# Perceiver layer on one core: x's keys as one product, softmax sums through DRAM, gating and late scan placed anew

## The chip, the cores and the metric

The kernel runs on one core of one Trainium2 chip. A core has TensorE (PE in the profile, with its weight loads as PEld), VectorE (DVE), ScalarE (ACT), GpSimd (POOL) and SyncE (SP), each with its own instruction stream that runs in order. The metric is the time of one execution on the device in microseconds; less is better.

## The reference, cut to what matters

One layer: cross-attention of 256 tokens of each of four batches to 4096 context tokens and to themselves, then a router that sends a quarter of the tokens of each batch to a small self-attention and the rest through a state-space model (SSM), then a mixture of experts. All in fp32.

```python
# x (4,256,256), ctx (4,4096,256); layernorm before each part, residual after it
q = split_heads(x1 @ Wq1)                        # 8 heads of 64
k = concat([x1 @ Wk1, ctx @ Wk2])                # 256 keys of x, 4096 of ctx
v = concat([x1 @ Wv1, ctx @ Wv2])
x = x + softmax(q @ k.T * 64**-0.5) @ v @ Wo + bo

score = gelu(xn @ r_w1 + r_b1) @ r_w2 + r_b2      # router
top 64 tokens of a batch: attention of 16 heads; the 192 others: SSM
    xc = silu(conv(xi)); h = exp(delta*A) * h + delta*xc*B; y = sum_s C*h   # 16 states

g, u = x @ w_gate[e].T, x @ w_up[e].T             # 8 experts, the best 2 per token
x = x + sum_e weight[e] * (silu(g) * u) @ w_down[e].T
```

## The kernel before, in words

**Attention.** The 4 batches times 4 head pairs make 16 groups G. A group has 8 steps s of 32 query rows, so 128 steps n in all; the loop from L1509 on writes out the order of every engine by hand, and each engine runs its instructions in that order. In a step, the products of `scores` fill the PSUM tile `su` with the scores of both heads j, each against the four quarters q of the keys: 1024 keys of ctx per quarter from `kt[r, q, lo : lo + 512]` (L1383, contraction over the 64 rows of one head) and 64 keys of x per quarter (L1391). For the latter, `qz` holds q with the other head's rows zero (`[P, 2, T]`, filled at L1351 by `k_self`), so that the contraction runs over all 128 rows. `copy_max` (L1403, DVE) copies the scores to SBUF and takes the maximum, `stat` (L1410, L1415, L1420) joins the maxima of the four quarters through a product, `exps` (L1431, ACT) takes the exponentials with their sums, `turn` (L1440, DVE) transposes them, and `values` (L1449, PE) multiplies by v four steps at a time. Between these lie pieces of the next group's work: `k_chunk` (keys, L1330), `v_chunk` (values, L1367), `k_self` (keys and queries of x).

At the end of a group, `sums` (in step s=0 of the next group) adds the parts of the softmax sums with a small product (L1463), takes the reciprocal `rl` (64 rows, 8 steps; L1468) and spreads it along a diagonal, `dg` (L1470). `spread` (at s=1) multiplies `dg` by the constant `pair`, which gives the reciprocals in PSUM as `psr`, one row per output channel and one column per query (L1477). `normalize` (L1492, DVE) multiplies the two halves of the attention output `ao` by it; `project` (L1496) follows.

**Work in the background.** Routers, small attentions and SSMs of finished batches are generators. They yield a delay and a budget in the time of a planner, `now`, which the loop moves on by a fixed cost for each piece that it places; `slot(budget)` places as many due items as the budget allows. So the planner's numbers set the order in the instruction streams, not the time on the chip. Batches 0 to 2 run beside the attention; batch 3 runs "late", beside the experts.

**Experts.** `ordered()` takes six of the eight token tiles, sorted by expert, in NB=19 blocks of 128: per block a gather of the tokens (`gather`, POOL), a turn (`turn_block`, PE L1723, ACT L1726), the gate products p0b and the up products p1b (both L1732, `half`, each 8 products), the gating `gated` (tanh on ACT L1678, then DVE `sg` L1679 and `hb` L1683), and the down products pdb of the block before (L1746, `down`) with their store `ysd` on ACT's queue (L1754). The PSUM tiles of the products come from a pool of three (`ps_g`). The last two tiles, those of batch 3, go through all experts densely (`experts()`, pg and pu L1868, pde L1881), once batch 3's router, attention and SSM are done. After each product half the loop adds its cost to `now` and calls `slot(5.0)`, which places the late work of batch 3: layernorm and router (psxn L250, psh L270, pssc L277), the ranks (two comparisons, one per half of the tokens; DVE), psn (L306 to L308), the gathering products psg (L331), psin (L626), then 16 pieces of the scan: `decay` on ACT (L805), and on DVE a product L838, the scan L839, a product L845 and a sum L846; `sums` adds a piece into the PSUM tile `yps` (L813). Then follow the SSM's output (pssd L871, psback L881) and the dense tiles' layernorm and transpose (`prepare`: x4l, psx L1824).

Of the kernel before, what the change touches and what calls it, by code (L numbers as in the profile page):

```python
# [8 lines left out]
F32 = mybir.dt.float32  # L9
# [5 lines left out]
P = 128  # L15
# [31 lines left out]
def perceiver_layer(ctx: ExitStack, tc: tile.TileContext, a: dict, out: bass.AP):  # L47
# [184 lines left out]
    def router(b, st):  # L232
# [55 lines left out]
        for h in range(2):  # L288
# [8 lines left out]
            if h == 0 and not late:  # L297
                yield 0.5, 1.6
# [4 lines left out]
        yield (4.5 if late else 1.0), 1.4  # L303
# [299 lines left out]
    def front_late(b, st, ws, conv):  # L603
# [73 lines left out]
        yield 5.4, 0  # L677
# [99 lines left out]
    def ssm_scan_late(b, st):  # L777
# [45 lines left out]
        zero = pool.tile([P, SG, NBOT], F32, tag="dbl", name="zero", bufs=4)[:, :2]  # L823
# [10 lines left out]
        for i in range(K * NDT):  # L834
            k, m = divmod(i, NDT)
            decay(i + 1)
            db = dbl[i] = pool.tile([P, SG, NBOT], F32, tag="dbl", name="db", bufs=4)
# [9 lines left out]
            if i:  # L847
                sums(i - 1)
# [4 lines left out]
            yield 3.9, 3.8  # L853
# [351 lines left out]
    with ExitStack() as s1:  # L1205
# [85 lines left out]
        def turn_x(b):  # L1291
# [11 lines left out]


        pair = fin.tile([2 * 32, P], F32, name="pair")
        nc.vector.tensor_copy(
            pair.rearrange("p (j d) -> p j d", j=2), bc(quarter[: 2 * 32, 0:2, 0], 2, HD)
        )
        qzs = [fin.tile([P, 2, T], F32, name=f"qz{i}") for i in range(2)]
        for t in qzs:  # L1310
            nc.gpsimd.memset(t, 0.0)
# [11 lines left out]
        def k_chunk(G, g):  # L1323
            b = G // NHP
            if G not in kts:
                kts[G] = wke.tile([P, 4, QK], F32, tag="kt", name="kt")
# [9 lines left out]
        def k_self(G):  # L1336
            x1T = x1Ts[G // NHP]
            if G not in kts:
                kts[G] = wke.tile([P, 4, QK], F32, tag="kt", name="kt")
# [7 lines left out]
            keys_out(G, SQ, ps[:, :T])  # L1347
            qTs[G] = qzs[G % 2]
            for j in range(2):
                r = slice(j * HD, (j + 1) * HD)  # L1350
                nc.scalar.activation(qTs[G][r, j, :], ps[r, T:], AF.Copy, scale=HD ** -0.5)  # L1351
# [24 lines left out]
        def scores(n):  # L1376
            G, s = divmod(n, 8)
            qT, kt = qTs[G], kts[G]
            for lo in range(0, SQ, 512):
                for q in range(4):  # L1380
                    for j in range(2):
# [3 lines left out]
                            qT[r, j, s * 32 : (s + 1) * 32], kt[r, q, lo : lo + 512],  # L1385
# [3 lines left out]
            for j in range(2):  # L1389
                for q in range(4):  # L1390
                    nc.tensor.matmul(  # L1391
                        su[q * 32 : (q + 1) * 32, SX[j] : SX[j] + QK - SQ],
                        qT[:, j, s * 32 : (s + 1) * 32], kt[:, q, SQ:],
                        start=True, stop=True,
                    )
# [60 lines left out]
        dgs, rss = {}, {}  # L1456

        def sums(G):
# [8 lines left out]
            rl = fin.tile([2 * 32, 8], F32, tag="rl", name="rl")  # L1467
            nc.vector.reciprocal(rl, ps[: 2 * 32, :8])  # L1468
            dgs[G] = fin.tile([2 * 32, 8, 32], F32, tag="dg", name="dg")
# [483 lines left out]
```

## Time and profile before

| | before |
|---|---|
| time, median of 3 runs (lowest to highest) | 1538.34 us (1537.46 to 1538.44) |
| profiled execution: its time, its span | 1534.16 us, 1532.4 us |
| mean granted TensorE clock in it | 0.984 |
| busy, PE / DVE / ACT / POOL | 1452.4 / 1062.5 / 758.1 / 411.9 us |
| PE instructions | 15686 |
| moved by DMA | 223.41 MB, mean 146 GB/s |

The span is the time from the first to the last instruction of the profiled execution. Attention takes it up to some 1245 us, its end and the last projection to 1273 us, and experts with batch 3's background work take the rest. Busy time is the sum of an engine's instructions; the slices cut the span in 40 equal parts of 38.3 us and give busy time in tenths. In a row of groups, "idle before" is time in which the engine stood still just before such an instruction, with the one that released it.

### The profile page before, as it was taken

Reading aid. Unit: us, or ns where it says so; the run is one execution under the profiler, and the core shown is the slowest. Engines: PE = TensorE matmul, PEld = TensorE weight load, DVE = VectorE, ACT = ScalarE, POOL = GpSimd, SP = SyncE. Lnnn points to the kernel's source line nnn. Section 1 sums busy time; section 2 is a strip of 40 time slices with the busy share of each in tenths; the row PEclk is TensorE's granted clock in tenths of the full one; section 3 lists DMA queues with packets and bytes.
Section 4 is the critical chain, followed back from the end, with each engine's and each line's share of the span. In section 5 each row is a group of like instructions: output and inputs, shape, how many; then the busy total and the mean of one; then the engine's idle time right before and its main releaser. Section 6 shows DMA issues by size and latency. Waiting matters only on the chain.

```text
span 1532.4 us, 37303 instructions
## 1 busy us (share of the span) xinstructions
PE 1452.4 (95%) x15686; PEld 1034.5 (68%) x15686; DVE 1062.5 (69%) x1825; ACT 758.1 (49%) x1484; POOL 411.9 (27%) x465
## 2 busy tenths in 40 slices
PE   7999999999999999999999999999998968899899
PEld 3657676677666566675756665757574757888687
DVE  1666665656589986565899956666999663689453
ACT  3444454455566645454766544656655523544211
POOL 1000000000069960000499800001999101210110
PEclk9999999999999999999999999999999979999999
DMA  6455434424345443424445444352643333788461
GB/s 229 142 158 152 157 116 150 154 85 131 109 145 179 138 131 121 148 82 144 144 135 174 135 134 130 103 163 73 182 157 99 105 131 109 244 272 283 136 203 49
DMA packets 157767, 223.41 MB, mean 146 GB/s; under 512 B 14976, under 2 KB 76160, under 8 KB 157600
## 3 DMA queue, kind: packets, MB, share of 16 engines
q1 hardware_dynamic: 149632, 208.96, 43.3%
q10 hardware_dynamic: 6480, 8.00, 1.6%
q0 software_dynamic: 1488, 4.07, 1.0%
q8 instruction: 124, 2.03, 0.5%
q14 instruction: 43, 0.35, 0.1%
HBM read 216.56 MB, written 4.42 MB: 144 GB/s over the span
## 4 chain that ended last, share of the span: by engine, by line
PE 65%; POOL 15%; DVE 11%; issue 4%; ACT 2%; DMA 1%; SPq 0%; ACTq 0%; DVEq 0%; POOLq 0%
PE po L1449 12%; PE su L1383 11%; PE psv L1367 11%; PE psk L1330 9%; POOL y L751 6%; POOL db L736 5%; POOL db L749 5%; DVE sp L1403 3%; PE su L1391 2%; PE pg L1868 2%; PE pu L1868 2%; PE pde L1881 2%; PE p1b L1732 2%; DVE db L743 1%; DVE pt L1440 1%
## 5 line engine op out<-in xcount | busy, mean ns | idle before, releaser
L1403 DVE TENSOR_SCALAR_CACHE_REDUCE sp<-su 128x1088 f32<-128x1088 f32 x256 | 318.8, 1282 | 181.9 <-PE su L1391 181.9
L1440 DVE STREAM_TRANSPOSE pt<-sp 128x1088 f32<-128x1088 f32 x256 | 328.0, 1295 | 57.4 <-PE po L1449 57.4
L1431 ACT ACTIVATE sp<-sp,nb 128x1088 f32<-128x1088 f32 x256 | 305.1, 1195 | 13.4 <-DVE nb L1420 13.2
L1449 PE MATMUL po<-pt,v 128*64 128x128 f32 x4352 | 261.9, 277 | 2.3 <-DVE pt L1440 1.3
L1383 PE MATMUL su<-kt,qz 64*32 64x512 f32 x4096 | 255.5, 607 | 4.4 <-DVE nb L1420 3.7
L1330 PE MATMUL psk<-ctx,wk 128*128 128x512 f32 x512 | 245.5, 612 | 10.5 <-DMA ctx<-in_ctxT 7.8
L1367 PE MATMUL psv<-wv,ctx 128*128 128x128 f32 x2048 | 250.3, 279 | 0.5 <-DMA ctx<-in_ctxT 0.3
L1449 PEld LDWEIGHTS po<-pt,v 128*64 128x64 f32 x4352 | 240.0, 138 | 13.9 <-issue 7.5
L1367 PEld LDWEIGHTS psv<-wv,ctx 128*128 128x128 f32 x2048 | 236.1, 192 | 6.6 <-issue 1.3
L1330 PEld LDWEIGHTS psk<-ctx,wk 128*128 128x128 f32 x512 | 91.4, 192 | 95.6 <-issue 86.0
L1318 ACT COPY kt<-psk 128x512 f32<-128x512 f32 x128 | 74.9, 585 | 157.7 <-PE psk L1330 157.5
L1383 PEld LDWEIGHTS su<-kt,qz 64*32 64x32 f32 x4096 | 63.3, 107 | 123.6 <-issue 94.3
L751 POOL TENSOR_TENSOR y<-y,db 128x192 f32<-128x192 f32 x192 | 135.5, 706 | 15.1
L1371 ACT COPY v<-psv 128x512 f32<-128x512 f32 x144 | 79.3, 558 | 119.4 <-PE psv L1367 118.0
L743 DVE TENSOR_TENSOR_SCAN db<-da,db 128x384 f32<-128x384 f32 x96 | 122.7, 1279 | 13.2 <-POOL db L736 2.5
L749 POOL TENSOR_TENSOR db<-db,cb 128x384 f32<-128x384 f32 x96 | 111.3, 1159 | 24.3 <-DVE da L741 24.3
L395 POOL TENSOR_TENSOR kbd<-qk,hmask 128x512 f32<-128x512 f32 x8 | 9.1, 1156 | 402.6 <-ACT qk L385 402.6
L736 POOL TENSOR_TENSOR db<-bb,xc 128x384 f32<-128x384 f32 x96 | 111.2, 1180 | 0.2
L1391 PEld LDWEIGHTS su<-kt,qz 128*32 128x32 f32 x2048 | 34.5, 109 | 108.9 <-issue 108.9
L731 ACT ACTIVATE da<-delta,A_log_sb 128x192 f32<-128x192 f32 x192 | 75.6, 447 | 52.7 <-DVE da L741 39.7
L1486 ACT COPY ao<-po 128x128 f32<-128x128 f32 x32 | 8.5, 264 | 149.8 <-PE po L1449 149.8
L1415 PEld LDWEIGHTS su<-mq,same 128*128 128x128 f32 x256 | 41.1, 192 | 54.8 <-DVE mq L1410 37.0
(298 smaller groups left out, 1582.1 us busy)
## 6 DMA issues: line engine op xcount, KB each, us to landing
ctx<-in_ctxT SPq DMA_DIRECT2D x256, 512.0 KB, 5.0
gateT<-in_gateT SPq DMA_DIRECT2D x27, 512.0 KB, 4.6
upT<-in_upT SPq DMA_DIRECT2D x27, 512.0 KB, 4.7
downT<-in_downT SPq DMA_DIRECT2D x27, 512.0 KB, 5.7
bb<-bcd SPq DMA_DIRECT2D x24, 192.0 KB, 3.8
cb<-bcd SPq DMA_DIRECT2D x24, 192.0 KB, 3.9
wv<-in_wv SPq DMA_DIRECT2D x32, 128.0 KB, 2.5
in_w<-in_in_w SPq DMA_DIRECT2D x32, 128.0 KB, 2.4
```

The costliest lines, as they stand in the source:

```text
L736: nc.gpsimd.tensor_tensor(db, bbs[k], bc(xc[:, m, :], 1, SG), ALU.mult)
L743: nc.vector.tensor_tensor_scan(out=db, data0=da, data1=db, initial=0.0, op0=ALU.mult, op1=ALU.add,)
L749: nc.gpsimd.tensor_tensor(db, db, cbs[k], ALU.mult)
L751: nc.gpsimd.tensor_tensor(y[:, m, :], y[:, m, :], db[:, s, :], ALU.add)
L1330: nc.tensor.matmul(ps, wqk[G][:, 0, c, :], ct[:, c, :], start=(c == 0), stop=(c == KD - 1),)
L1367: nc.tensor.matmul(ps[:, i * P : (i + 1) * P], lhsT, wv[G][:, w, c, :], start=(c == 0), stop=(c == KD - 1),)
L1371: nc.scalar.copy(v.rearrange("p k d -> p (k d)"), ps[:, : n * P])
L1383: nc.tensor.matmul(su[q * 32 : (q + 1) * 32, SC[j] + lo : SC[j] + lo + 512], qT[r, j, s * 32 : (s + 1) * 32], kt[r, q, lo : lo + 512], sta ...
L1403: nc.vector.tensor_scalar(out=sps[n][j], in0=su[:, SU[j] : SU[j] + QK], scalar1=1.0, scalar2=None, op0=ALU.mult, op1=ALU.max, accum_out=nm ...
L1431: nc.scalar.activation(sps[n][j], sps[n][j], AF.Exp, bias=nbs[n][:, j : j + 1], accum_out=lss[b][:, hp, s, j : j + 1],)
L1440: nc.vector.transpose(pts[m, j][:, i, :], sps[n][j])
L1449: nc.tensor.matmul(pos[m][j * HD : (j + 1) * HD, :], vts[m // 2, k // 4][:, k % 4, j * HD : (j + 1) * HD], pts[m, j][:, :, kk * 32 : (kk + ...
```

## The change

It has six parts.

1. q is kept unpadded (`qh`), and the keys of x go to zero-padded tiles `kxs`, one block of columns per head. One product per quarter then gives the scores of both heads, 128 columns wide, written with a stride through `middle` to the places in `su` where they lay before. `kt` holds the keys of ctx alone.
2. The reciprocals of the sums no longer go through `dg`, `pair` and a product. `sums` transposes `rl` in blocks of 32x32 on DVE, `spread` (now at s=0) writes it to a DRAM tile `rd` with two DMAs on ACT's queue, and the new `fetch` (at s=1) reads it back, each head's row repeated over its 64 partitions, into the SBUF tile `rs` which `normalize` reads.
3. In `ordered()`, the tanh and `sg` are placed after the first half of the up products instead of after all of them and the start of `down`; only the product `hb` stays there.
4. `ordered()` is started, up to its first turn, before the slot that precedes the blocks.
5. The late ranks are placed in two parts, with delays of 0.9 and 2.7 in place of one of 4.5.
6. The late scan starts after 3.6 instead of 5.4, its pieces are 3.5 apart instead of 3.9, each piece's `sums` come two pieces later instead of one, and the buffers `dbl` are five instead of four.

```diff
@@ -294,13 +294,13 @@
             nc.vector.tensor_reduce(out=rank[:, h : h + 1], in_=eq, axis=AX.X, op=ALU.add)
-            if h == 0 and not late:
-                yield 0.5, 1.6
+            if h == 0:
+                yield (0.9 if late else 0.5), 1.6
         top = small.tile([P, 2], F32, name="top")
...
         )
-        yield (4.5 if late else 1.0), 1.4
+        yield (2.7 if late else 1.0), 1.4
@@ -674,7 +674,7 @@
         next(st["late"])
-        yield 5.4, 0
+        yield 3.6, 0
         u = st["u"] = pool.tile([P, NDT, NBOT], F32, tag="ul", name="ul")
@@ -820,7 +820,7 @@
         yps = st["yps"] = late["psum"].tile([P, 2, 512], F32, name="yps")
-        zero = pool.tile([P, SG, NBOT], F32, tag="dbl", name="zero", bufs=4)[:, :2]
+        zero = pool.tile([P, SG, NBOT], F32, tag="dbl", name="zero", bufs=5)[:, :2]
         nc.gpsimd.memset(zero, 0.0)
@@ -834,7 +834,7 @@
             decay(i + 1)
-            db = dbl[i] = pool.tile([P, SG, NBOT], F32, tag="dbl", name="db", bufs=4)
+            db = dbl[i] = pool.tile([P, SG, NBOT], F32, tag="dbl", name="db", bufs=5)
             nc.vector.tensor_tensor(db, spread[k, 0], bc(u[:, m, :], 1, SG), ALU.mult)
@@ -844,13 +844,14 @@
             nc.vector.tensor_tensor(db[:, : SG // 2], db[:, : SG // 2], db[:, SG // 2 :], ALU.add)
-            if i:
-                sums(i - 1)
+            if i > 1:
+                sums(i - 2)
             if m == NDT - 1:
...
                 start(gate_late(b, st))
-            yield 3.9, 3.8
+            yield 3.5, 3.8
+        sums(K * NDT - 2)
         sums(K * NDT - 1)
@@ -1301,13 +1302,12 @@
-        pair = fin.tile([2 * 32, P], F32, name="pair")
-        nc.vector.tensor_copy(
-            pair.rearrange("p (j d) -> p j d", j=2), bc(quarter[: 2 * 32, 0:2, 0], 2, HD)
-        )
-        qzs = [fin.tile([P, 2, T], F32, name=f"qz{i}") for i in range(2)]
-        for t in qzs:
+        middle = su[:, SX[0] : SX[0] + 2 * (SX[1] - SX[0])].rearrange("p (j k) -> p j k", j=2)
+        qhs = [fin.tile([P, T], F32, name=f"qh{i}") for i in range(2)]
+        kxs = [fin.tile([P, 4, 2, QK - SQ], F32, name=f"kx{i}") for i in range(2)]
+        for t in kxs:
             nc.gpsimd.memset(t, 0.0)
@@ -1323,7 +1323,7 @@
             if G not in kts:
-                kts[G] = wke.tile([P, 4, QK], F32, tag="kt", name="kt")
+                kts[G] = wke.tile([P, 4, SQ], F32, tag="kt", name="kt")
             ct = load_ctx(b, g)
@@ -1335,8 +1335,6 @@
             x1T = x1Ts[G // NHP]
-            if G not in kts:
-                kts[G] = wke.tile([P, 4, QK], F32, tag="kt", name="kt")
             ps = ps_m.tile([P, 512], F32, tag="m", name="psks")
@@ -1344,11 +1342,14 @@
                     )
-            keys_out(G, SQ, ps[:, :T])
-            qTs[G] = qzs[G % 2]
+            qTs[G] = qhs[G % 2]
+            nc.scalar.activation(qTs[G], ps[:, T:], AF.Copy, scale=HD ** -0.5)
             for j in range(2):
                 r = slice(j * HD, (j + 1) * HD)
-                nc.scalar.activation(qTs[G][r, j, :], ps[r, T:], AF.Copy, scale=HD ** -0.5)
+                nc.scalar.copy(
+                    kxs[G % 2][r, :, j, :].rearrange("p q (k i) -> p q k i", i=32),
+                    ps[r, :T].rearrange("p (k q i) -> p q k i", q=4, i=32),
+                )
@@ -1382,17 +1383,16 @@
                             su[q * 32 : (q + 1) * 32, SC[j] + lo : SC[j] + lo + 512],
-                            qT[r, j, s * 32 : (s + 1) * 32], kt[r, q, lo : lo + 512],
+                            qT[r, s * 32 : (s + 1) * 32], kt[r, q, lo : lo + 512],
                             start=True, stop=True,
...
-            for j in range(2):
-                for q in range(4):
-                    nc.tensor.matmul(
-                        su[q * 32 : (q + 1) * 32, SX[j] : SX[j] + QK - SQ],
-                        qT[:, j, s * 32 : (s + 1) * 32], kt[:, q, SQ:],
-                        start=True, stop=True,
-                    )
+            for q in range(4):
+                nc.tensor.matmul(
+                    middle[q * 32 : (q + 1) * 32, :, : QK - SQ],
+                    qT[:, s * 32 : (s + 1) * 32], kxs[G % 2][:, q],
+                    start=True, stop=True,
+                )
@@ -1453,7 +1453,10 @@
-        dgs, rss = {}, {}
+        rts, rds, rss = {}, {}, {}
+        rls = [fin.tile([2 * 32, 32], F32, name=f"rl{i}") for i in range(2)]
+        for t in rls:
+            nc.gpsimd.memset(t, 0.0)
@@ -1464,18 +1467,25 @@
                 )
-            rl = fin.tile([2 * 32, 8], F32, tag="rl", name="rl")
-            nc.vector.reciprocal(rl, ps[: 2 * 32, :8])
-            dgs[G] = fin.tile([2 * 32, 8, 32], F32, tag="dg", name="dg")
-            nc.vector.tensor_tensor(
-                dgs[G], bc(rl, 2, 32), bc(dm[: 2 * 32, :], 1, 8), ALU.mult
-            )
+            rl = rls[G % 2]
+            nc.vector.reciprocal(rl[:, :8], ps[: 2 * 32, :8])
+            rts[G] = fin.tile([2 * 32, 32], F32, tag="rt", name="rt")
+            nc.vector.transpose(rts[G], rl)
...
-            rss[G] = bank("psr")[:, :T]
-            nc.tensor.matmul(
-                rss[G], pair, dgs[G].rearrange("p s i -> p (s i)"), start=True, stop=True
+            rd = dram.tile([2, 8, 32], F32, tag="rd", name="rd")
+            for j in range(2):
+                nc.scalar.dma_start(out=rd[j], in_=rts[G][j * 32 : j * 32 + 8, :])
+            rds[G] = rd
+        def fetch(G):
+            rss[G] = fin.tile([P, T], F32, tag="rs", name="rs")
+            nc.scalar.dma_start(
+                out=rss[G],
+                in_=rds[G].rearrange("j s i -> j (s i)").unsqueeze(1).to_broadcast([2, HD, T]),
             )
@@ -1594,13 +1604,14 @@
                     piece(2)
+                    if s == 0 and n:
+                        spread(G - 1)
                     slot(2.9)
...
                     last = s == 1 and G
+                    slot(1.5)
                     if last:
-                        spread(G - 1)
-                        now[0] += 0.6
-                    slot(1.5)
+                        fetch(G - 1)
                     piece(1)
@@ -1672,7 +1683,7 @@
-        def gated(pg, pu, out, n):
+        def silu(pg, n):
@@ -1680,7 +1691,10 @@
             )
-            nc.vector.tensor_tensor(out, sg[:, :n], pu[:, :n], ALU.mult)
+            return sg
+        def gated(pg, pu, out, n):
+            nc.vector.tensor_tensor(out, silu(pg, n)[:, :n], pu[:, :n], ALU.mult)
@@ -1760,10 +1774,19 @@
             turn_block(0)
+            yield 0.0
             for j in range(NB):
...
                 load(j + 3, 0)
-                pu = yield from half(j, 1)
+                up = half(j, 1)
+                yield next(up)
+                sg = silu(pg, 512)
+                try:
+                    while True:
+                        yield next(up)
+                except StopIteration as end:
+                    pu = end.value
                 load(j + 3, 1)
@@ -1771,7 +1794,9 @@
                 hs[j] = fk.tile([P, NHC, P], F32, name="hb")
-                gated(pg, pu, hs[j].rearrange("p m i -> p (m i)"), 512)
+                nc.vector.tensor_tensor(
+                    hs[j].rearrange("p m i -> p (m i)"), sg, pu, ALU.mult
+                )
                 yield from rest
@@ -1894,9 +1919,11 @@
         late["prepare"] = prepare
+        blocks = ordered()
+        next(blocks)
         now[0] += 1.0
         slot(5.0)
-        for took in ordered():
+        for took in blocks:
             now[0] += took
```

## The prediction

> **What bounds the kernel now.** I read the engine totals and the slices first, then the chain, then the groups by form, then the timeline of one attention step and of the tail.
>
> ```profile
> PE 1452.4 (95%) x15686; PEld 1034.5 (68%) x15686; DVE 1062.5 (69%) x1825; ACT 758.1 (49%) x1484; POOL 411.9 (27%) x465
> PE   7999999999999999999999999999998968899899
> POOL 1000000000069960000499800001999101210110
> PE 65%; POOL 15%; DVE 11%; issue 4%; ACT 2%; DMA 1%; SPq 0%; ACTq 0%; DVEq 0%; POOLq 0%
> ```
>
> TensorE is at work in 95% of the span. So there are two ways to gain: give PE less to do, or fill its idle time (80 us). POOL's 15% of the chain lies in the three stretches where its slices read 9: the scans of batches 0 to 2 beside the attention. There a wait can end on VectorE or POOL, and a shorter PE may gain nothing. Listing the gaps between PE records after 1273 us gives 20.2 us of idle in the tail (experts, with batch 3's scan beside them). The waits name most of it:
>
> ```profile
> PE p1b L1732 <- DVE sg L1679: 7.2, 5, 3.5
> PE psx L1824 <- ACT x4l L211: 3.6, 2, 3.4
> PE yps L813 <- DVE db L846: 3.4, 1, 3.4
> ```
>
> An attention step, at the turn of a group (s=0 to s=1, timeline at 300 us):
>
> ```profile
> 309.39 0.43 PE L1391 MATMUL su<-kt,qz 128*32 128x64 f32 x16
> 309.75 2.19 PE L1449 MATMUL po<-pt,v 128*64 128x128 f32 x36
> 311.87 0.70 PE L1477 MATMUL psr<-dg,pair 64*128 64x256 f32 x2
> 312.50 2.19 PE L1449 MATMUL po<-pt,v 128*64 128x128 f32 x36
> 315.12 0.28 DVE L1492 TENSOR_TENSOR ao<-ao,psr 128x128 f32<-128x128 f32 x1
> 318.57 1.95 PE L1383 MATMUL su<-kt,qz 64*32 64x512 f32 x32
> 318.75 2.50 DVE L1440 STREAM_TRANSPOSE pt<-sp 128x1088 f32<-128x1088 f32 x2 [3.35 <-PE po L1449]
> ```
>
> PE goes from product to product without a pause. `normalize` runs at 315.12, and VectorE's next work, the turns, can't begin before PE has ended `po` at 318.6.
>
> **The change part by part.** Durations are from the profiled execution: 1534.16 us, span 1532.4, 1.8 us around it. It lies 4.2 us below the median of the runs, 1538.34; I sum against 1534.16 and carry the difference to the median.
>
> *1. x's keys in one product.* The rows are
>
> ```profile
> L1391 PE MATMUL su<-kt,qz 128*32 128x64 f32 x2048 | 55.1, 225 | 0.0
> L1383 PE MATMUL su<-kt,qz 64*32 64x512 f32 x4096 | 255.5, 607 | 4.4 <-DVE nb L1420 3.7 <-ACT qz L1351 0.7
> L1351 ACT ACTIVATE qz<-psks 64x256 f32<-64x256 f32 x32 | 12.1, 378 | 0.3
> ```
>
> fp32 products are two records each. Per step 16 records of 64 columns take 309.39 to 309.75 = 0.36 us, in four waves of four column tiles; the change makes 8 records of 128 columns, two waves. Columns streamed: 4x64 before, 2x128 after, the same. L1383 gives the price of a column: 32 records in 1.87 us (307.52 to 309.39), eight at a time, so 4 x 512 columns, 0.91 ns each, 0.12 us per 128. By columns the old step is 0.23 us and 0.13 of start and drain, and the new step is again 0.36: gain 0. By count of waves (0.09 each) it would be 0.18: gain 0.18 x 128 steps = 23 us. The Trainium skill has a rule here, "TensorEngine Tiling (Array Packing)", section "Instruction Overhead": each product has about 60 cycles of overhead, so that one of 1 column lasts as long as one of 60. At 64 columns the old products are just above that floor, so by the rule too streaming sets the time, gain 0, if the overheads of the four column tiles overlap; if they add, most of the 23 us. The two ends are far apart; the nearest row is L1383, which goes by columns. I take 2 us (0.015 a step, one wave start less), keep 0 to 23. A loss is excluded on PE: no column or record more. ACT per group: one `kt` copy (364 ns) and two `qz` (378) become one `qh` of the first form and two `kx` of the second, 1.12 us before and after. Clearing kxs for qz is on POOL once, at the start.
>
> *2. Sums through memory.* Off PE: psr, 311.87 to 312.50 = 0.63 us a group, x16 = 10.1 us, all of it in PE's line of work. Off DVE: dg (507 ns), on DVE a 64x32 transpose; its own row doesn't exist, but the 128x1088 one is 1295 ns for 17 times the elements and twice the partitions, so 0.1 to 0.2 us; 0.3 us saved, worth nothing by itself. `normalize` reads SBUF instead of PSUM, 261 ns kept. On ACT's queue come three DMA issues, two writes (8 rows of 128 bytes) at s=0 and the fetch at s=1; ACT's issues in this trace are 0.34 us (`ysd`, `bcd`), so 1.0 us a group. Behind the writes on ACT stand the exponentials of n-1 (308.1 to 311.6): 0.7 us later, they end at 312.3, and the turns that read them don't start before 318.75. Hidden. If rt were late they would wait for it, but the reciprocal is done at 305.9 and ACT comes to the writes after 307.6. The fetch waits for the writes' landing in ACT's in-order queue; nothing due stands behind it until the copy of `ao` at 318.72. The planner's shift of 0.6 us for psr goes with it; in the attention it moves no other instruction.
>
> Then the landing. The new wait is `normalize` for rs, and behind it on DVE stand both turns, the next copy_max and mq, for which PE's L1415 waits (already its largest wait, 18.9 us in 14 times). The fetch is issued at about 312.4 and must have landed by 318.4: 6 us. How long does it take? Rows:
>
> ```profile
> wv<-in_wv SPq DMA_DIRECT2D x32, 128.0 KB, 2.5
> bb<-bcd SPq DMA_DIRECT2D x24, 192.0 KB, 3.8
> ctx<-in_ctxT SPq DMA_DIRECT2D x256, 512.0 KB, 5.0
> ```
>
> The same 128 KB as wv: 2.5 us. But a rule of the Trainium skill speaks against it: "DMA: Bandwidth & Descriptors", section "Why a DMA increments its semaphore by 16 and not by 1", says that the number of engines is the largest, up to 16, that divides the slowest dimension of both access patterns. The fetch's source has 2 (head), then 64 (repeat), then 256: two engines with 64 packets of 1 KB each. Packets of 1 KB take 46 to 49 ns in this trace, so 3 us in a row instead of 0.4: landing 2.5 + 2.6 = about 5 us by the rule, 2.5 by the row; no run here shows which. With ctx traffic on the same two engines it is up to 8. At 5 us it lands at 317.4, and `normalize` ends 1 us before the turns can start: nothing is lost in a quiet group. In the six groups whose psr lies in POOL's stretches (475.6, 548.8, 792.3, 865.6, 1110.7, 1182.0) DVE has no pause there, so half of their 0.63 is taken to be lost: 1.9. At the attention's end psr ran at 1261.9 and `normalize` right behind it, with `project` waiting (psx at 1264.6); writes and fetch in a row end between 1262 and 1266: 1 us lost (0 to 3). Sum: -10.1 + 1.9 + 1 = -7.2; bounds -10 to +14 (1.3 us a group lost, were landing 8 us).
>
> *3. Gating in two steps.* p1b waits for DVE's sg because p0b's bank comes free late (three banks). The tanh and the first product now come after a quarter of `up` instead of after all of it, some 1.3 us earlier in PE's order, and DVE reads p0b before the scan pieces that stood ahead of it. DVE's work is the same two products (682 and 688 ns). Of the five waits (3.53, 1.53, 1.30, 0.46, 0.38) all may go: -7.2.
>
> *4. Start of the blocks, ranks, scan pieces.* `next(blocks)` ahead of a slot puts the first turn's copy before a table load: 1.96 us idle at 1273 gone, but psxn then waits for xn: -0.6. Ranks in two: psn, which needs `top` from DVE, goes ahead of psxb and pdb on PE and waits for it: +2.5 (0 to 3.5), and the branch's front is 3 us earlier. Sums two pieces behind instead of one: the 3.37 us wait for db goes (there POOL's kbd stretched two DVE operations from 0.96 and 0.56 to 1.61 and 1.28 us; with another piece between that is covered). About three expert blocks now lie behind the last piece, 5.5 us of PE each, and cover the chain pssd, psback, x4l: 0.87 + 0.46 + 3.40 + 0.17 + 0.68 = -5.6. In return the scan is denser: a piece comes every 4 planner steps rather than 5. A piece is 0.95 + 1.76 + 0.97 + 0.56 = 4.3 us of DVE, and two thirds of a block beside it 0.9: 5.2 us of DVE against about 4.3 of PE. DVE, 88 of 97 us busy there before, becomes the bound:
>
> ```profile
> 1330.00:1427.00 97.00, 89.29 (x643) 82.64 (x643) 88.06 (x99) 40.91 (x107) 11.29 (x10) 0.98 0.86 275
> ```
>
> (PE, PEld, DVE, ACT, POOL.) From the first of yps to the last sum I count 16 x 4.3 and eleven blocks of 1.4 and some 4 to 6 of the rest, 88 to 90 us of DVE, against 84 to 86 of PE: +6 (3 to 12). Sum of parts 3 and 4: -7.2 - 0.6 + 2.5 - 3.4 - 5.6 + 6 = -8.3, range -14 to 0. No DMA is added in parts 3 and 4; the expert loads keep their order on SP, and the gathers on POOL move with their blocks.
>
> Total: -2 - 7.2 - 8.3 = -17.5: 1516.7 for the profiled execution, 1521 on the median's scale.
>
> **The rivals.** (a) The fetch lands late. Each us beyond the slack is lost in every group, as DVE holds turns, copy_max and mq behind it. The slack is 318.4 - 312.4 = 6 us and 0.4 to 0.5 that DVE has before mq. Parts 1, 3, 4 and psr bring about 20 us; it is slower than before once a group loses over 1.25 us, so from a landing of about 7.7 us after the issue. At 9 us: 2.5 x 16 = 40, less 20, 1558. For it: two engines, and ctx streams at 43% of all engines' time. Against it: the share of DMA at 311 to 320 us is 0.03, the loads lie before. (b) The tail gives nothing: DVE-bound pieces and psn eat what gating gains; 1521 + 8 = 1529. For it: DVE's 88 of 97. Against: three blocks as cover behind the scan. (c) The x keys go by count: 23 instead of 2, 1500. Against: L1383's columns. (d) Edits without effect on the order of work would leave all as it was, 1538; the removed products make that unlikely.
>
> **How the numbers follow.** My forecast, 1521 (own range 1513 to 1530): 0.63. (b) 1529, up to 1537 with some late landings: 0.17, of which 0.06 ends within 0.2% of before (3.1 us, about what this kernel's measurement can tell from no change). (a) 0.14, of which 0.01 within; (c) 0.05; (d) 0.01. Faster 0.79, same 0.08, slower 0.13. The range is 1507 to 1537: it leaves out (a) and (c).
>
> **What would show it.** L1391's group with 1024 records and about 45 us where the starts in a step stay 0.36 apart (right) or 0.18 (c); no psr, and po records 0.6 us closer at the group's turn; rs landing 5 us after its issue, no wait "ao <- DMA rs" that grows L1415's 18.9 us by more than 5 (else (a)); no p1b wait for sg, yps waits of 0.3 to 0.8 us at most pieces (above 12 us in sum: (b)); no gap before psx L1824. PE's busy time should fall by about 12 us and its idle time by about 5.

## The result, and the profile after

| | before | after |
|---|---|---|
| time, median of 5 runs (lowest to highest) | 1538.34 us (1535.15 to 1540.35) | 1526.89 us (1523.21 to 1532.38) |
| ratio to before, 95% interval | | 0.9939 (0.9916 to 0.9963) |
| span of the profiled execution | 1532.4 us | 1525.1 us |
| mean granted TensorE clock in it | 0.984 | 0.981 |

The kernel is 11.4 us faster by the medians, 9.4 by the ratio. The forecast was 17.3, so between half and two thirds of it came.

The page of after, engine totals and chain:

```profile
PE 1444.4 (95%) x14630; PEld 1021.4 (67%) x14630; DVE 1061.7 (70%) x1824; ACT 758.6 (50%) x1484; POOL 404.5 (27%) x467
PE 60%; DVE 20%; POOL 9%; issue 5%; DMA 3%; ACT 2%; SPq 0%; ACTq 0%; DVEq 0%; POOLq 0%
```

PE has 1056 records less and 8 us less to do, but its share of the span is the same 95%: its idle time did not shrink. DVE, 11% of the chain before, is 20% of it now. The view of waits says where (times are the total, the count, the longest):

```profile
DVE ao L1502 <- DMA rs<-rd: 35.8, 13, 6.5
PE su L1415 <- DVE mq L1410: 27.4, 19, 3.4
PE p0b L1746 <- ACT xTb L1740: 6.5, 3, 3.2
PE psn L306 <- DVE top L300: 1.7, 1, 1.7
PE yps L813 <- DVE db L846: 0.8, 1, 0.8
PE p1b L1746 <- DVE sg L1690: 0.5, 1, 0.5
```

The waits that the change was to take away are gone: p1b for sg from 7.2 to 0.5 us, yps for db from 3.4 to 0.8, psx for x4l (3.6) no longer in the list. Two have grown: L1415 for mq by 8.5 us, p0b for xTb by 3.4. And the new wait for rs stands at 35.8 us. Most of it is DVE time that nobody misses; the experiments find the part that is missed.

One attention step with no scan beside it (timeline):

```profile
305.78 1.95 PE L1384 MATMUL su<-kt,qh 64*32 64x512 f32 x32
...
307.65 0.43 PE L1391 MATMUL su<-kx,qh 128*32 128x128 f32 x8
...
308.01 4.15 PE L1449 MATMUL po<-pt,v 128*64 128x128 f32 x72
...
309.78 0.51 ACTq L1486 DMA_DIRECT2D rs<-rd  x1
...
312.09 0.30 PEld L1415 LDWEIGHTS su<-mq,same 128*128 128x128 f32 x2 [0.17 <-issue]
...
314.58 0.29 DVE L1502 TENSOR_TENSOR ao<-ao,rs 128x128 f32<-128x128 f32 x1 [1.90 <-DMA rs<-rd]
...
316.05 0.18 PEld L1384 LDWEIGHTS su<-kt,qh 64*32 64x32 f32 x16 [0.17 <-issue]
...
316.22 2.51 DVE L1440 STREAM_TRANSPOSE pt<-sp 128x1088 f32<-128x1088 f32 x2 [1.35 <-PE po L1449]
```

The products of x's keys still take 307.65 to 308.01 = 0.36 us. psr is gone from between the `po` products: from the first of them to L1415 it is 4.08 us, and was 4.86 before (309.75 to 314.61), so 0.78 us a group. rs lands in time: `normalize` is done 1.3 us before the turns can start. This much is as forecast.

### The profile page after: what moved, and what is told of

Its sections match the earlier page's. It is cut to its first block, busy times and chain, and to the rows that moved or that the text cites. A ratio compares the mean times of both kernels' runs of the same rounds, so it can differ in the third digit from the quotient of the medians.

```text
span 1525.1 us, 35283 instructions
## 1 busy us (share of the span) xinstructions
PE 1444.4 (95%) x14630; PEld 1021.4 (67%) x14630; DVE 1061.7 (70%) x1824; ACT 758.6 (50%) x1484; POOL 404.5 (27%) x467
## 4 chain that ended last, share of the span: by engine, by line
PE 60%; DVE 20%; POOL 9%; issue 5%; DMA 3%; ACT 2%; SPq 0%; ACTq 0%; DVEq 0%; POOLq 0%
PE psv L1368 10%; PE su L1384 10%; PE po L1449 10%; PE psk L1330 9%; DVE sp L1403 6%; DVE db L743 4%; POOL y L751 3%; POOL db L749 3%; POOL db L736 3%; DVE pt L1440 3%; PE su L1391 2%; PE pde L1906 2%; PE pg L1893 2%; PE pu L1893 2%; DVE db L839 2%
## 5 line engine op out<-in xcount | busy, mean ns | idle before, releaser
L1431 ACT ACTIVATE sp<-sp,nb 128x1088 f32<-128x1088 f32 x256 | 305.1, 1195 | 15.7 <-DVE nb L1420 13.8
L1384 PE MATMUL su<-kt,qh 64*32 64x512 f32 x4096 | 256.3, 610 | 4.5 <-DVE nb L1420 4.0
L1449 PEld LDWEIGHTS po<-pt,v 128*64 128x64 f32 x4352 | 242.4, 139 | 11.9 <-issue 6.3
L1384 PEld LDWEIGHTS su<-kt,qh 64*32 64x32 f32 x4096 | 63.1, 108 | 124.0 <-issue 95.5
L751 POOL TENSOR_TENSOR y<-y,db 128x192 f32<-128x192 f32 x192 | 139.7, 728 | 15.0
L743 DVE TENSOR_TENSOR_SCAN db<-da,db 128x384 f32<-128x384 f32 x96 | 126.4, 1317 | 11.4 <-POOL y L751 0.5
L749 POOL TENSOR_TENSOR db<-db,cb 128x384 f32<-128x384 f32 x96 | 108.1, 1126 | 43.6 <-DVE da L741 43.6
L731 ACT ACTIVATE da<-delta,A_log_sb 128x192 f32<-128x192 f32 x192 | 75.4, 447 | 51.0 <-DVE da L741 31.5
L736 POOL TENSOR_TENSOR db<-bb,xc 128x384 f32<-128x384 f32 x96 | 99.5, 1059 | 0.2
L1391 PEld LDWEIGHTS su<-kx,qh 128*32 128x32 f32 x1024 | 20.2, 108 | 109.4 <-issue 109.4
L1415 PEld LDWEIGHTS su<-mq,same 128*128 128x128 f32 x256 | 40.8, 190 | 66.3 <-DVE mq L1410 46.9
```

Of the source, the lines that this page charges most:

```text
L736: nc.gpsimd.tensor_tensor(db, bbs[k], bc(xc[:, m, :], 1, SG), ALU.mult)
L743: nc.vector.tensor_tensor_scan(out=db, data0=da, data1=db, initial=0.0, op0=ALU.mult, op1=ALU.add,)
L749: nc.gpsimd.tensor_tensor(db, db, cbs[k], ALU.mult)
L751: nc.gpsimd.tensor_tensor(y[:, m, :], y[:, m, :], db[:, s, :], ALU.add)
L1384: nc.tensor.matmul(su[q * 32 : (q + 1) * 32, SC[j] + lo : SC[j] + lo + 512], qT[r, s * 32 : (s + 1) * 32], kt[r, q, lo : lo + 512], start= ...
L1431: nc.scalar.activation(sps[n][j], sps[n][j], AF.Exp, bias=nbs[n][:, j : j + 1], accum_out=lss[b][:, hp, s, j : j + 1],)
```

## The experiments

Every kernel was timed in five rounds beside runs of before; the ratio is to those. Two theories of what went missing in the attention were held against each other. A: in the groups with a scan beside them, `normalize` waits for a fetch that is issued late, and what stands behind it on DVE is late too. B: the scan's own pace on POOL and DVE ends those stretches, so a shorter PE is worth nothing there.

**x's keys alone.** Edit of before:

```diff
-            for j in range(2):
-                for q in range(4):
-                    nc.tensor.matmul(
-                        su[q * 32 : (q + 1) * 32, SX[j] : SX[j] + QK - SQ],
-                        qT[:, j, s * 32 : (s + 1) * 32], kt[:, q, SQ:],
...
+            for q in range(4):
+                nc.tensor.matmul(
+                    middle[q * 32 : (q + 1) * 32, :, : QK - SQ],
+                    qT[:, s * 32 : (s + 1) * 32], kxs[G % 2][:, q],
```

> Before, with x's keys in one product and nothing else of the change. Theory (columns set the time): 1024 records in L1391's group instead of 2048, but 0.36 us per step from the first of them to the next product, as before; the time is that of before within 2 us (1536 to 1540). Rival (count sets it): 0.18 us per step, 1515.

Measured: 1538.63 us against 1538.40, ratio 0.9997 (0.9981 to 1.0013). The group by form:

```profile
L1393 PE MATMUL su<-kx,qh 128*32 128x128 f32 x1024 | 55.0, 287 | 0.0
```

Half the records, the same 55 us of busy time (before: 55.1). At these widths, 64 and 128 columns, the columns set the time of the products, not their number. This part of the change is worth nothing that these runs can tell.

**Sums through memory alone.** Edit of before:

```diff
-            rss[G] = bank("psr")[:, :T]
-            nc.tensor.matmul(
-                rss[G], pair, dgs[G].rearrange("p s i -> p (s i)"), start=True, stop=True
+            rd = dram.tile([2, 8, 32], F32, tag="rd", name="rd")
+            for j in range(2):
+                nc.scalar.dma_start(out=rd[j], in_=rts[G][j * 32 : j * 32 + 8, :])
...
+        def fetch(G):
...
+                in_=rds[G].rearrange("j s i -> j (s i)").unsqueeze(1).to_broadcast([2, HD, T]),
```

> Before, with the sums through memory and nothing else. Theory A (order on ACT): outside the scan stretches each group gains about 0.75 us at its turn; in groups 6, 10 and 14, where a scan runs, the fetch stands on ACT behind exponentials of the scan that wait for DVE, normalize comes 2 us late and PE then waits some 3 us for mq; about -3 us at the end of the attention, 1535. Theory B (the scan's own pace): the gain is lost in the scan stretches because POOL's pieces (3.9 us each) end them, whatever normalize does; also about 1535. Telling them apart is fetch_first's task; this run tells what of the gain belongs to the sums: 1535 if the tail brings the other 4 us of the profile, 1528 if nearly all comes from here.

Measured: 1534.51, ratio 0.9968 (0.9949 to 0.9988), 3.9 us less. The trace shows the same waits as after's, among them 36.3 us of DVE for rs. It also shows a gain that nobody had expected. Before had

```profile
PE psat L437 <- ACT ev L586: 4.3, 3, 1.4
...
PE psas L419 <- ACT projT L560: 1.5, 3, 0.5
```

in its waits, and so has the kernel with the keys alone; here and in after both are gone. `bank()` hands out PSUM tiles of one tag in turn. psr took one per group, and without it the small attention's products come to other tiles than those that ACT is still reading. That is my reading of the code; shown is that the 5.8 us go with psr.

**The tail's four edits alone.** Edit of before: the diff's hunks on gating, blocks, ranks and scan, and none on the attention.

> Before, with the tail's four edits (gating in two steps, blocks started earlier, ranks in two, scan pieces denser) and the attention as before. If the profile of after reads right: 4 us less, 1534, with p1b's wait for sg (7.2 us before) below 1 and new waits of p0b for xTb of about 6 us. If the attention's new end had been what moved the tail: within 1 us of before.

Measured: 1530.55, ratio 0.9952 (0.9935 to 0.9970), 7.9 us less by the medians. By the traces the stretch from pstok to the end went from 1532.4 - 1248.5 = 283.9 to 1532.7 - 1253.3 = 279.4 us, 4.5 less. The three parts (+0.2, -3.9, -7.9) add up to -11.6, beside the -11.4 of the whole.

**fetch ahead of the scan's exponentials.** In the groups where a scan runs, the timeline of after reads:

```profile
465.66 1.95 PE L1384 MATMUL su<-kt,qh 64*32 64x512 f32 x32
...
470.63 0.79 ACT L731 ACTIVATE da<-delta,A_log_sb 128x192 f32<-128x192 f32 x2
...
474.21 0.46 ACT L731 ACTIVATE da<-delta,A_log_sb 128x192 f32<-128x192 f32 x1 [2.80 <-DVE da L741]
474.39 0.52 ACTq L1486 DMA_DIRECT2D rs<-rd  x1
...
478.79 0.99 DVE L1502 TENSOR_TENSOR ao<-ao,rs 128x128 f32<-128x128 f32 x1 [2.28 <-DMA rs<-rd]
...
479.70 2.49 DVE L1440 STREAM_TRANSPOSE pt<-sp 128x1088 f32<-128x1088 f32 x2
...
484.89 0.37 DVE L1410 TENSOR_TENSOR mq<-nm,quarter 128x8 f32<-128x8 f32 x1
...
485.31 0.39 PE L1415 MATMUL su<-mq,same 128*128 128x8 f32 x2 [2.86 <-DVE mq L1410]
```

Read it downwards. `slot(1.5)` places the scan's exponentials (L731) on ACT ahead of fetch, and one of them waits 2.80 us for a memset on DVE. So fetch goes out 8.7 us after the step began (474.39 - 465.66), where in the quiet step it was 4.0. DVE is free at 476.5 and waits for rs until 478.79; the turns start at 479.70 although PE had ended `po` at 476.4; mq is late, and PE stands for 2.86 us. With the start of each step's first L1384 subtracted from that of before, the lead of after shrinks at this place by 3.1, 4.0 and 4.1 us in groups 6, 10 and 14, one in each scan. (In the last two a phase of 3.4 us at half the clock reaches into the step, from 801.8 and from 1119.2 us on, and takes 0.9 and 1.1 us of that; the clock comes up again under "How sure".) Edit of after:

```diff
-                    slot(1.5)
                     if last:
                         fetch(G - 1)
+                    slot(1.5)
                     piece(1)
```

> After, with fetch placed on ACT before the slot(1.5) of s=1 instead of behind it, so before the scan's exponentials. Theory A: fetch is issued up to 3.5 us earlier in the groups with a scan beside them, the wait of normalize for rs falls from 35.8 us to below 25, the lost 3 to 4 us at step 2 of groups 6, 10 and 14 come back: 7 to 10 us less than after, about 1518. Theory B: no change beyond 1.5 us, 1527. If the landing alone were at fault, the wait for rs would stay near 2 us a group, and the time too.

Measured: 1518.80, ratio 0.9875 (0.9853 to 0.9897): 8 us less than after. The waits:

```profile
DVE ao L1502 <- DMA rs<-rd: 19.8, 9, 6.9
PE su L1415 <- DVE mq L1410: 24.5, 22, 3.4
```

A holds. But in groups 6, 10 and 14 the step still loses 1.8 us each.

**fetch as two DMAs, the repeat outermost.** Edit of after:

```diff
-            nc.scalar.dma_start(
-                out=rss[G],
-                in_=rds[G].rearrange("j s i -> j (s i)").unsqueeze(1).to_broadcast([2, HD, T]),
-            )
+            for j in range(2):
+                nc.scalar.dma_start(
+                    out=rss[G][j * HD : (j + 1) * HD, :],
+                    in_=rds[G][j : j + 1].rearrange("j s i -> j (s i)").to_broadcast([HD, T]),
+                )
```

> After, with fetch at its place but as two DMAs, one per head, so that the slowest dimension is 64 (repeat) and not 2 (head). By the rule on engines each uses 16 of them, 4 packets of 1 KB per engine instead of 64: last packet 1.3 + 0.2 to 0.5 us after its issue, so some 2 to 2.6 us after the first issue instead of 4.0 to 4.6. Theory A (normalize late on DVE where a scan runs): normalize's wait for rs falls from 35.8 to about 10 us, the late groups 6, 10, 14 win some 1.7 us each and steps after them likewise: 1520 to 1523. If the landing had no part in it: 1527. If two engines were not the reason for 4 us: packets end at 4 us again.

Measured: 1517.32, ratio 0.9866 (0.9839 to 0.9893), 9.6 us less than after. In the packet records of after, the first packet of a fetch starts 1.3 us after the issue and the last ends at 4.0 to 4.6 (5.3 once): 128 packets of 46 ns in the median. On two engines 64 of them in a row are 2.9 us, and 2.7 to 3.3 passed between the first and the last. Here the second DMA's last packet ends 2.1 to 2.6 us after its issue (3.2 once), and up to 8 packets are on their way at once, where it was 3 or 4 in after. The edit changes two things, the shape and the number of DMAs, and no run tells them apart. The wait for rs fell less than expected:

```profile
DVE ao L1503 <- DMA rs<-rd: 15.7, 10, 3.3
```

since in six of the ten groups without a scan the second issue comes 1.3 to 1.9 us after the first, with ACT idle (0.55 us in the other four): I read it as the wait for the second write, as the single fetch had it. That part costs nothing.

**normalize behind the turns.** This leaves fetch and its landing alone and takes only what is queued behind `normalize`: both halves now stand between the turns and the next `copy_max`. Edit of after:

```diff
-                    if last:
+                    if last and n == N + 1:
                         normalize(m - 1)
...
                     if last:
+                        if n <= N:
+                            normalize(m - 1)
                         normalize(m)
```

> After, with fetch and its landing as they are, but normalize(m - 1) placed on DVE behind both turns (except at the very end of the attention). Theory A (what costs is what stands behind the waiting normalize on DVE): the turns no longer wait for rs, and the 2.3 to 3 us lost at step 2 of groups 6, 10 and 14 mostly come back: 1518 to 1521, as with fetch_first. If a late rs cost through something else (ACT's queue, the engines of the DMA): 1526.

Measured: 1517.65, ratio 0.9870 (0.9844 to 0.9895), 9.2 us less than after. Timeline of the same step:

```profile
471.72 0.46 ACT L731 ACTIVATE da<-delta,A_log_sb 128x192 f32<-128x192 f32 x1 [2.79 <-DVE da L741]
...
471.90 0.52 ACTq L1486 DMA_DIRECT2D rs<-rd  x1
...
473.89 1.95 PE L1384 MATMUL su<-kt,qh 64*32 64x512 f32 x32
474.06 2.50 DVE L1440 STREAM_TRANSPOSE pt<-sp 128x1088 f32<-128x1088 f32 x2
...
476.49 1.81 DVE L1502 TENSOR_TENSOR ao<-ao,rs 128x128 f32<-128x128 f32 x2
...
478.23 1.28 DVE L1403 TENSOR_SCALAR_CACHE_REDUCE sp<-su 128x1088 f32<-128x1088 f32 x1
...
481.54 0.39 PE L1415 MATMUL su<-mq,same 128*128 128x8 f32 x2 [1.58 <-DVE mq L1410]
```

fetch is as late as before, and it no longer matters: the turns start right behind the scan piece, and PE's wait is 1.58 instead of 2.86 us. So the cost lay in what stood behind `normalize` on DVE, not in the DMA as such.

What is left, 1.8 us at each of these steps, was to be B's: no turn waits for rs here. The traces show something else. The same step before:

```profile
482.28 0.26 DVE L1492 TENSOR_TENSOR ao<-ao,psr 128x128 f32<-128x128 f32 x1
482.34 1.95 PE L1383 MATMUL su<-kt,qz 64*32 64x512 f32 x32
...
482.51 2.51 DVE L1440 STREAM_TRANSPOSE pt<-sp 128x1088 f32<-128x1088 f32 x2
...
484.94 0.25 DVE L1492 TENSOR_TENSOR ao<-ao,psr 128x128 f32<-128x128 f32 x1
485.11 1.28 DVE L1403 TENSOR_SCALAR_CACHE_REDUCE sp<-su 128x1088 f32<-128x1088 f32 x1
...
488.25 0.29 PE L1415 MATMUL su<-mq,same 128*128 128x8 f32 x2
```

and in best_1 (further below), where rs has landed in time:

```profile
475.59 1.95 PE L1384 MATMUL su<-kt,qh 64*32 64x512 f32 x32
475.65 1.03 DVE L1503 TENSOR_TENSOR ao<-ao,rs 128x128 f32<-128x128 f32 x1
476.61 2.49 DVE L1440 STREAM_TRANSPOSE pt<-sp 128x1088 f32<-128x1088 f32 x2
...
479.03 0.93 DVE L1503 TENSOR_TENSOR ao<-ao,rs 128x128 f32<-128x128 f32 x1
479.88 1.28 DVE L1403 TENSOR_SCALAR_CACHE_REDUCE sp<-su 128x1088 f32<-128x1088 f32 x1
...
483.18 0.39 PE L1415 MATMUL su<-mq,same 128*128 128x8 f32 x2 [1.52 <-DVE mq L1410]
```

From the step's first product of scores to `copy_max` it is 2.77 us before, 4.29 in best_1 and 4.34 in norm_late. Nearly all of the 1.5 us in between is `normalize` itself: 1.03 and 0.93 us (1.81 for both in norm_late), where it took 0.26 and 0.25. PE did not wait for mq before and waits 1.52 and 1.58 us now; groups 10 and 14 read the same. So at this step it is a slower `normalize` that is left, not the scan's pace; what slows it stands in the last section. B was not shown for any step, and no run tests it elsewhere.

Over a whole scan, POOL's pieces (L736, from the second on) of the first scan start 8.0 us earlier than before (421.9 against 429.9) and end 5.4 earlier (545.7 against 551.1), 2.6 us lost; in after they start 5.6 earlier and end 2.1 earlier, 3.5 lost. Over the three scans after gives back 9.4 us of this lead and norm_late 4.5.

**Gating alone; ranks and scan alone.** Edit of before, first kernel:

```diff
-                pu = yield from half(j, 1)
+                up = half(j, 1)
+                yield next(up)
+                sg = silu(pg, 512)
...
```

> Before, with the gating in two steps alone. p1b's waits for sg (7.2 us in 5 times) should fall below 1. If all of them are saved: 1531. If the wait only moves to where DVE next holds PE (hb for pdb, db for yps), as theory B of a DVE-bound scan has it: 1536 to 1538.

Measured: 1533.24, ratio 0.9975 (0.9961 to 0.9989). From pstok to the end it takes 280.0 us, 3.9 less than before. All of p1b's 7.2 us are gone, but

```profile
PE p0b L1735 <- ACT xTb L1729: 6.5, 4, 2.6
PE pdb L1749 <- issue: 1.6, 1, 1.6
PE pdb L1749 <- ACT zs L634: 0.9, 1, 0.9
```

p0b's wait was 3.1 before, and the two of pdb are new. Nearly half of the 7.2 us comes back as other waits. Second kernel, edit of before:

```diff
-            if h == 0 and not late:
-                yield 0.5, 1.6
+            if h == 0:
+                yield (0.9 if late else 0.5), 1.6
...
-        yield 5.4, 0
+        yield 3.6, 0
...
-            if i:
-                sums(i - 1)
+            if i > 1:
+                sums(i - 2)
...
-            yield 3.9, 3.8
+            yield 3.5, 3.8
```

> Before, with the ranks in two parts and the scan's new distances, lag and buffers, gating as before. The end of the scan comes earlier and x4l's wait of 3.4 us goes, and that of yps for db (3.4) too, but p1b waits for sg more often as the pieces stand closer: 1533 to 1536. If the denser scan alone were what brings the tail's gain: 1531; if it needs the early gating: 1538 or above.

Measured: 1540.50, ratio 1.0013 (0.9997 to 1.0030). From pstok to the end it is 286.3 us, 2.4 more than before:

```profile
PE p1b L1733 <- DVE sg L1680: 12.3, 5, 4.1
```

The waits for x4l and db went as meant, but pieces that stand closer keep DVE's `sg` back, and p1b waits 12.3 us instead of 7.2. The two balance: PE is idle for 28.6 us from pstok to the end, and was for 28.1. The 2.4 us are no more than what the granted clock took there, 15.1 us against 12.2 (half of the time that it stood at 0.50). So without the early gating the denser scan brings nothing; that it costs something is not shown, as the interval holds 1.

**Towards a faster kernel.** First, both cures of fetch, and the late scan's loads one piece later. In after, the issue of `cbl` on ACT waited at 1336.8 to 1339.7 for DVE's L845 to free its buffer, with a tanh and xTb's copy behind it and PE 2.66 us behind that. Edit of after, besides those of fetch_first and fetch_16:

```diff
-            if m == NDT - 1:
-                load(k + 2)
+            if m == 0 and k:
+                load(k + 1)
```

> After, with fetch before slot(1.5), as two DMAs, and with the late scan's loads of B and C issued one piece later, so that the issue on ACT doesn't wait for DVE's product L845 with xTb's copy behind it. fetch_first took 8 us off after; the loads should take the wait of p0b for xTb from 6.6 to about 3.5 us, and an earlier landing 1 to 3 more: 1513 to 1517. If DVE's work in the late scan is the bound, the wait that is removed comes back as another and it stays at 1517 to 1519.

Measured: 1513.53, ratio 0.9840 (0.9817 to 0.9862), the lowest median of all, with an interval that overlaps those of fetch_first, fetch_16, norm_late, best_2 and best_3. Its waits:

```profile
PE p0b L1747 <- ACT xTb L1741: 4.8, 3, 3.2
DVE ao L1503 <- DMA rs<-rd: 5.4, 2, 3.3
```

Second, on top of it, the table loads of `ev` out of xTb's way:

```diff
+        yield 0.9, 0
         nc.scalar.activation(ev, ev, AF.Exp, scale=-1.0)
         nc.scalar.activation(ev, ev, AF.Ln, bias=1.0)
         next(st["late"])
-        yield 3.6, 0
+        yield 2.7, 0
```

> best_1, with the late exponential and logarithm of ev (two table loads of 1.28 us on ACT) placed one planner step later, so that the copy of xTb goes ahead of them and p0b doesn't wait 3.2 us for it. If that wait is the last one there: 1510 to 1511. If the scan's start moves back by as much as the copy moves ahead (DVE is the bound of the late scan): 1513 to 1515.

Measured: 1514.92, ratio 0.9859 (0.9834 to 0.9884): no gain. p0b's longest wait for xTb was 3.2 us and is 4.7, now at the next block: the same work on ACT, one block later.

Third, both cures of the late `normalize` at once, with the later loads:

> After, with both cures of the late normalize (fetch before slot(1.5), normalize(m - 1) behind the turns; fetch a single DMA) and the late scan's loads one piece later. If both cure the same wait, they don't add: the attention ends as in norm_late, the tail as in best_1, 1511 to 1514. If a wait for rs was left in norm_late or fetch_first that counts: 1508 to 1510.

Measured: 1515.43, ratio 0.9868 (0.9849 to 0.9886). They don't add: pstok starts at 1235.4 us, and at 1236.3 and 1236.9 with the one cure (norm_late) and the other (fetch_first). So they cure one and the same wait.

Last, without the denser scan. The edit of before is the attention's two parts with both changes of fetch, and the gating:

> Both attention edits with fetch before slot(1.5) and as two DMAs, and the gating in two steps; the start of the blocks, the ranks and the late scan as before. In the traces gating alone took 3.8 us off the tail and all four edits 4.4. If the denser scan is worth only that 0.6 us: about 1517, some 0.5 to 1 us above the kernel that has all four edits without the later loads (fetch_16's 1517 less up to 1). If it brings the 3 to 4 us that the medians of the runs hint at (tail_only 1530.6 against gating_only 1533.2): 1519 to 1521.

Measured: 1520.49, ratio 0.9889 (0.9866 to 0.9912). From pstok to the end 1519.5 - 1238.7 = 280.8 us, against 278.1 in fetch_16 (1516.3 - 1238.2), which has the start, ranks and scan of after. The median fits a worth of 3 us, but the intervals overlap, and in the traces PE's idle time differs by 0.6 us (24.1 against 23.5) and what the clock took by 2.3 (14.1 against 11.8). That the new start, ranks and denser scan gain anything beside the gating is not shown.

## Why the prediction was right in sign and too large

| part | forecast | measured |
|---|---|---|
| 1, x's keys | -2 (0 to -23) | +0.2, interval -2.9 to +2.0 |
| 2, sums | -7.2 (-10 to +14) | -3.9, interval -7.8 to -1.8 |
| 3 and 4, tail | -8.3 (-14 to 0) | -7.9 by the medians, -4.5 by the traces |
| all | -17.5 | -11.4, interval -12.9 to -5.7 |

*Part 1.* The row of L1383 was the right one, and so was what the rule of the Trainium skill gave with overlapping overheads ("TensorEngine Tiling (Array Packing)", section "Instruction Overhead"): nothing. The 2 us for a wave start less did not show.

*Part 2, PE's side.* The 0.63 us were 0.78. (On DVE, the 128x1088 transpose has 34 times the elements per partition of the new one, not 17; it took 0.20 us, the upper end of what was said.) Not in the sum at all were the 5.8 us of psat and psas: psr was priced as time on PE, and not as the holder of a PSUM tile.

*Part 2, the landing.* "About 5 us by the rule, 2.5 by the row": the fetch's last packet ended at 4.0 to 4.6 us and `normalize` began 4.4 to 5.1 us after the issue in the quiet groups. The rule of the Trainium skill ("DMA: Bandwidth & Descriptors", section "Why a DMA increments its semaphore by 16 and not by 1") held against the row of wv: 128 packets of 46 ns in 2.7 us are 2.2 at a time, which fits two engines. fetch_16, with another shape and two DMAs, was done in 2.1 to 2.6 us. So rival (a) did not come as it was put: no landing was near 7.7 us.

*Part 2, the step that failed:* "The fetch is issued at about 312.4". I asked what stands behind the fetch on ACT and found nothing due. I did not ask what `slot(1.5)` puts ahead of it. In groups 6, 10 and 14 that is exponentials that wait for DVE, and the fetch is issued 8.5 to 8.7 us into the step instead of 4.0. The queue behind `normalize` that the prediction lists for rival (a) then did just what was said there. A second step failed beside it: "`normalize` reads SBUF instead of PSUM, 261 ns kept". Beside POOL's scan it took up to 1.03 us.

"Half of their 0.63 is taken to be lost: 1.9" was the term that was mis-sized. At the three steps PE waits 2.9 us each for mq in after, 1.5 to 1.6 with either cure and not at all before: so 1.3 us each for the late fetch, and nearly all of the rest for the slower `normalize`. By POOL's pieces after gives back 9.4 us in the three scans, of which norm_late gets 4.9 back. By the medians the late fetch costs 8 to 9.6 us in all; the table under "How sure" shows where: PE's idle time falls by 4 to 6 us, and the granted clock takes 3 to 5 us less.

*Parts 3 and 4.* "Of the five waits all may go: -7.2": they went (0.5 us is left), but gating alone brought 3.9 in its trace, as p0b and pdb took over part of the waiting. psn cost 1.7 (forecast 2.5). The chain to x4l was covered, as forecast. The denser scan's +6 is 10.7 us of PE idle in 1310 to 1409, listed from the gaps:

```profile
1310.00:1409.00 99.00, 88.28 (x608) 80.56 (x608) 89.81 (x107) 49.18 (x123) 16.79 (x13) 0.97 0.81 258
```

DVE is at work for 89.8 of the 99 us, as worked out; but the two longest gaps, 3.2 and 2.7 us, come from ACT's order (table loads, and a DMA issue that waits for DVE), which the prediction hadn't looked at.

*How sure.* The attention of before is in four traces (before and the three kernels that change only the tail), and pstok starts at 1248.5, 1249.5, 1253.0 and 1253.3 us. So one and the same program differs by 5 us there between executions. The granted clock goes with it. The clock record of a trace stands at 1.00, broken by phases of 3.4 us (or twice that) at 0.50; half of such a phase is lost. From the first product of scores to pstok, in us:

| | before | scan_only | tail_only | gating_only | after | fetch_16 | fetch_first | norm_late |
|---|---|---|---|---|---|---|---|---|
| time | 1222.0 | 1223.9 | 1227.6 | 1227.8 | 1220.7 | 1213.5 | 1211.4 | 1210.9 |
| PE idle | 44.4 | 45.3 | 45.7 | 44.2 | 49.9 | 46.0 | 45.2 | 44.3 |
| lost at half clock | 12.4 | 14.2 | 17.3 | 19.0 | 17.1 | 13.8 | 11.9 | 11.9 |

The first four have the same attention: their idle time is the same within 1.5 us, and the last row follows the first. Most of the difference between before and tail_only falls into one stretch, here in that order (the 0.96 and 0.87 are the clock):

```profile
1159.00:1199.00 40.00, 35.34 (x421) 22.63 (x421) 37.24 (x58) 19.04 (x39) 33.23 (x37) 0.96 0.31 96
1159.00:1199.00 40.00, 34.02 (x394) 20.38 (x395) 36.11 (x58) 17.45 (x37) 33.98 (x39) 0.87 0.22 74
```

The timed runs agree: of the 72 of before, the nine at a mean clock of 0.978 have a median of 1540.6 us, the eleven at 0.982 one of 1534.9. This is why the tail's size is taken from within a trace, and why medians and traces differ by some us: the runs of tail_only have a median clock of 0.982, those of before 0.979. What starts a phase, and how many of them a change itself brings, these runs do not show. In after against the cured kernels it may well be the waits, as all five runs of after lie at 0.977 to 0.982 and all of norm_late at 0.982 to 0.985; that is a guess.

## What to carry to other kernels

For a step that is moved to another engine's queue, ask on that queue both ways: what waits behind it, and what that waits for something else is placed ahead of it. A DMA whose result is consumed in order belongs ahead of any work that can stall, and its consumer behind any work that could have run without it; either cure was enough here. Before a difference between two traces is put down to an edit, the granted clock of the stretch belongs beside it. And a small product costs more than its time: it also takes its turn in a rotation of PSUM tiles.

## What the runs showed of the hardware that was not expected

`normalize` reads rs from SBUF where it read psr from PSUM; its other operand, ao, is in SBUF in both. Before, the twelve that ran in POOL's scans took 0.25 to 0.26 us, no more than in a quiet step. In after the twelve in the scans took 0.30 to 1.03 us, and those outside 0.25 to 0.29. POOL's instruction at that moment can be the same: at 482.28 before (0.26 us) and at 475.65 in best_1 (1.03 us) it was at L749. The group by form of after:

```profile
L1502 DVE TENSOR_TENSOR ao<-ao,rs 128x128 f32<-128x128 f32 x32 | 13.4, 420 | 40.8 <-DMA rs<-rd 35.8 <-ACT ao L1496 4.9
```

420 ns in the mean, where L1492 had 261. So with both operands in SBUF this instruction is slowed while POOL is at work, up to four times, and with one of them in PSUM it is not. It is small in sum (5 us of DVE), but at the three steps shown under norm_late PE waits for it, 1.5 us each.
